# Attention output projection of the second pass: from one level of seven products to two, over pairs of key/value groups

## The chip, the cores and the metric

The kernel runs on one core of one Trainium2 chip. The metric is device time in microseconds (us) of one execution. A core has five engines that run side by side and wait for each other by semaphores: PE (TensorE, the matrix products; PEld is its weight load), DVE (VectorE), ACT (ScalarE), POOL (GpSimd) and SP (SyncE, which here issues DMA transfers). A profile of one execution shows when each instruction ran.

## The reference

The reference is two layers of a gated network over x of 8 sequences of 256 tokens, 1024 wide, in fp32. The part that matters is the second layer's attention, with 32 query heads and 8 key/value heads (so 8 groups of 4 query heads), all heads 128 wide:

```python
q = (query @ wq).reshape(bs, s, N_Q_HEADS, D_K).transpose(0, 2, 1, 3)
k = (key @ wk).reshape(bs, s, N_KV_HEADS, D_K).transpose(0, 2, 1, 3)
v = (value @ wv).reshape(bs, s, N_KV_HEADS, D_V).transpose(0, 2, 1, 3)
q = _rope(q)
k = _rope(k)
qg = q.reshape(bs, N_KV_HEADS, g, s, D_K)
scores = jnp.einsum('bhgqd,bhkd->bhgqk', qg, k) / scale
masked = jnp.where(mask[:, None, None].astype(bool), scores, -1000000000.0)
w = jax.nn.softmax(masked, axis=-1)
out = jnp.einsum('bhgqk,bhkd->bhgqd', w, v)
out = out.reshape(bs, N_Q_HEADS, s, D_V).transpose(0, 2, 1, 3).reshape(bs, s, N_Q_HEADS * D_V)
return out @ wo
...
x = x + jnp.tanh(g_xattn[1]) * _L1_xattn_ref(_layernorm(x, axis=-1), ctx_4096, ctx_4096, ...)
```

The change concerns `out @ wo`, the product of 4096 columns of attention output with the 4096 x 1024 matrix `wo`.

## The kernel before

The kernel makes two passes (`NPASS`), each over four sequences, that is 1024 rows of x, which stay on chip as eight tiles of 128 rows. A pass has four stages: an autocorrelation layer with the keys and values of the later attention computed beside it, a feed-forward layer (`lora_ffn`), the attention, and a second feed-forward layer (`fourier_ffn`).

Most large products use the seven-product scheme for 2 x 2 block matrices (Winograd's form): in place of eight block products there are seven, whose operands are sums of blocks (`left_operands`, `right_operands`) and whose results are added into the four result blocks. The products are named 1, 2, 6, 7, 4, 5, 3 and run in this order (`SEVEN`). Product 1 opens a running sum u, products 2, 6, 7, 5 and 3 add to it or to its copy w, and product 5 is used twice.

The attention runs 16 steps in each pass: two blocks of 512 rows (two sequences) by eight groups. A step k has four units (n, l): n is the sequence, l a half of the group's four heads. In each unit:

- `scores` multiplies queries by keys (line 977), then masks (986), reduces (988), exponentiates on ACT (991) and scales (1000) the weights of two heads.
- `values`, for the unit before, transposes the weights (1012), multiplies by the values (1023) and copies the result to a tile oT (1031).
- In between, PE is given other products from two generators: `queries` (929), the seven query products of the next step, and `outputs` (958), the seven output products of the step before. `q_fill` and `o_fill` (lines 1046 and 1047) say how many of each fall into each unit.

One output product of a step is [two row tiles] x [256 of the step's 512 columns of attention output] x [512 of the 1024 result columns]: two matmuls of 128 x 512 for each of the two row tiles. So a step has 7 x 2 x 2 = 28 matmuls. The result in PSUM is scaled by the gate and added into x or a partial sum by `add_product` (257 to 267, and `residual`, 375), on ACT, DVE and POOL.

Operands of the left side are made by POOL from the oT tiles (206 to 209). Operands of the right side are sums of blocks of `wo`: in the first block of the first pass they are made on chip by DVE and stored in DRAM (`wo_d`), and in the other blocks loaded (`load_wo`), seven tiles of 512 KB a step, into a group of seven buffers (`go`). `wq` is treated in the same way (group `gq`). PSUM tiles of the query and output products come from one pool of four buffers (`at_mm`).

`combine` evicts the query products and hands four finished blocks to `rope`, which multiplies them by tables on DVE (720 to 722) and adds on POOL (723).

The program is written in one order and then put into a fixed order for each engine's queue by a scheduler at build time; each queue runs in that order and waits where it must. SP issues nearly all DMA transfers.

Of the kernel before, what the change touches and what calls it, by code (L numbers as in the profile page):

```python
# [11 lines left out]
F32 = mybir.dt.float32  # L12
# [34 lines left out]
def flamingo_kernel(ctx: ExitStack, tc: tile.TileContext, a: dict, out: bass.AP):  # L47
# [26 lines left out]
    tab = const.tile([P, 2, S], F32, name="tab")  # L74
# [4 lines left out]
    def load_constants():  # L79
        nc.sync.dma_start(tab, a["rope"])  # L80
# [20 lines left out]
    ]  # L101

# [117 lines left out]
    def combine(r, ps, tiles, new, dest):  # L220
# [11 lines left out]
        elif r == 7:  # L232
            tiles["w"] = new("w")
            nc.vector.tensor_add(tiles["w"], ps, tiles["u"])
        elif r == 5:
# [478 lines left out]
    def rope(dst, ps, cos, sin, pool):  # L714

        H = P // 2
        t0 = pool.tile([P, 2, S], F32, tag="rope0", name="rope0", bufs=1)
        t1 = pool.tile([P, 2, S], F32, tag="rope1", name="rope1", bufs=1)
        tab = lambda t: t.unsqueeze(1).to_broadcast([t.shape[0], 2, S])
        nc.vector.tensor_mul(t0, ps, tab(cos))  # L720
        nc.vector.tensor_mul(t1[0:H], ps[H:P], tab(sin[H:P, :]))
        nc.vector.tensor_mul(t1[H:P], ps[0:H], tab(sin[0:H, :]))  # L722
        nc.gpsimd.tensor_add(dst, t0, t1)  # L723

    def keys_values(n, groups, pools):
# [105 lines left out]
    def query_operands(xt, norm, pool, ps_t, tag):  # L831
# [4 lines left out]
        for t in range(NBT):  # L836
            xn = pool.tile([P, D], F32, tag="xn", name="xl")
# [8 lines left out]
        return right_operands(nc.vector, q, *s)  # L846

# [3 lines left out]
    def attention(p, xt, gq, go, keep, norms, xops):  # L851
        with (
# [7 lines left out]
            wq, wo, kv = {}, {}, {}  # L860

# [22 lines left out]
            def load_wo(step):  # L884
# [12 lines left out]
                else:  # L897
                    ops = {}
                    where = {1: a["wo"][g, 0, 0], 2: a["wo"][g, 1, 0], 3: a["wo"][g, 1, 1]}
                    where |= dict(zip((5, 7, 6, 4), wo_d[g]))  # L900
                    for r in SEVEN:
                        ops[r] = big_tile(go, [2, HALF], f"wo_{r}")
                        nc.sync.dma_start(ops[r], where[r])
                wo[step] = ops

            def load_kv(step):
                blk, g = step
                r0 = p * BP * S + blk * NB
                kT = w2.tile([P, NB], F32, tag="kv", name="kT", bufs=4)
                nc.sync.dma_start(kT, kT_d[g, :, r0 : r0 + NB])  # L910
                v = w2.tile([P, NBT, DH], F32, tag="kv", name="v", bufs=4)
# [9 lines left out]
            def queries(step, qT):  # L921
# [3 lines left out]
                for r in SEVEN:  # L925
# [10 lines left out]
                    done = combine(r, ps, tiles, lambda tag: half(tag, 1), lambda: half("c", 2))  # L936
                    if done:
                        qT[done[1]] = half("qT", 8)
                        rope(qT[done[1]], done[0], tab_q[:, 0, :], tab_q[:, 1, :], w1)
                    yield  # L940

            def outputs(step, ops):
# [11 lines left out]
                for r in SEVEN:  # L954
                    for t in range(2):
# [10 lines left out]
                        add_product(r, po, x[t], tg_x[1], ntg_x[1], flat)  # L966
                    yield
# [38 lines left out]
            def values(step, l, n, got, oT, fill):  # L1006
# [23 lines left out]
                oT[n][l] = half("oT", 8)  # L1030
# [5 lines left out]

            load_wq(steps[0])
# [6 lines left out]
            last, before, nothing = None, None, iter(())  # L1044

            q_fill = {0: (2, 2, 1, 1), len(steps) - 1: (0, 0, 0, 0)}
            o_fill = {len(steps) - 1: (2, 2, 2, 1)}
            oT = [[None, None], [None, None]]
            for k, step in enumerate(steps):
# [9 lines left out]
                o_gen = nothing  # L1059
                for i, (n, l) in enumerate(((0, 0), (0, 1), (1, 0), (1, 1))):  # L1060
                    got = scores(step, l, n, qT)
                    nq = q_fill.get(k, (3, 3, 1, 0))[i]
                    no = o_fill.get(k, (0, 1, 3, 3))[i]
                    fill_from(q_gen, nq)
                    if i > 0:
                        fill_from(o_gen, no - 1)
                    if before is not None:
                        values(*before, lambda: fill_from(o_gen, 1 if no else 0))
                    before = step, l, n, got, oT
                    if i == 0 and k > 0:  # L1070
                        s = [half(f"oS{j}", 1) for j in (1, 2, 4)]
                        o_gen = outputs(last[0], left_operands(nc.gpsimd, last[1], *s))
                        fill_from(o_gen, no)
# [6 lines left out]
                    if i == 0:  # L1080
                        load_wo(step)
                for gen in (q_gen, o_gen):
                    for _ in gen:
                        pass
# [278 lines left out]
```

## Time and profile before

| | us |
|---|---|
| median of 3 runs | 3401.2 (3400.71 to 3402.15) |
| the profiled execution | 3396.83 |
| its span, first to last instruction | 3395.0 |
| second pass's attention, first query product to last output product | 2226.5 to 3281.9 |
| one step in the middle of it | 65.65 |
| output products after the last step | 22.6 |

In the lines of the profile a group is written: line, engine, operation, out<-in, shape and count; then its busy time in us and the mean of one in ns; then the idle time of its engine just before it and what ended that. A matmul of these fp32 operands appears as two records. The chain of waits is followed back from the last instruction: each piece is the work, or the wait, that held up the next one. Pieces in order of time give start, length and what ran. A table by windows gives the busy time of each engine in a stretch of time.

The page lists 160526 packets and 425.17 MB on the queue that SP feeds, 36.3% of the time of 16 DMA engines.

### The profile page before, as it was taken

Reading aid. Unit: us, or ns where it says so; the run is one execution under the profiler, and the core shown is the slowest. Engines: PE = TensorE matmul, PEld = TensorE weight load, DVE = VectorE, ACT = ScalarE, POOL = GpSimd, SP = SyncE. Lnnn points to the kernel's source line nnn. Section 1 sums busy time; section 2 is a strip of 40 time slices with the busy share of each in tenths; the row PEclk is TensorE's granted clock in tenths of the full one; section 3 lists DMA queues with packets and bytes.
Section 4 is the critical chain, followed back from the end, with each engine's and each line's share of the span. In section 5 each row is a group of like instructions: output and inputs, shape, how many; then the busy total and the mean of one; then the engine's idle time right before and its main releaser. Section 6 shows DMA issues by size and latency. Waiting matters only on the chain. (4 is left out here: it accounts for less than half of the span.)

```text
span 3395.0 us, 36926 instructions
## 1 busy us (share of the span) xinstructions
PE 3314.1 (98%) x12784; PEld 2279.1 (67%) x12784; DVE 2252.4 (66%) x4229; ACT 859.7 (25%) x2061; POOL 1354.6 (40%) x1213
## 2 busy tenths in 40 slices
PE   8899999999999999999999999999999999999999
PEld 6566546767767776775467766577767776776654
DVE  7787666877777666665657775556666666666563
ACT  1233111322222222222123321112222322222220
POOL 4665212344443443344335542123443444344332
PEclk9999999999999999999999999999999999999999
DMA  7433634333333333343153424053333333333411
GB/s 270 170 115 102 207 115 155 130 140 127 137 127 131 121 119 123 118 155 118 56 196 130 147 96 146 17 173 115 118 125 120 115 118 121 121 118 122 158 44 50
DMA packets 161864, 431.72 MB, mean 127 GB/s; under 512 B 21476, under 2 KB 56292, under 8 KB 161678
## 3 DMA queue, kind: packets, MB, share of 16 engines
q1 hardware_dynamic: 160526, 425.17, 36.3%
q0 software_dynamic: 1152, 4.19, 0.3%
q8 instruction: 102, 1.67, 0.2%
q14 instruction: 84, 0.69, 0.1%
HBM read 350.66 MB, written 78.64 MB: 126 GB/s over the span
## 5 line engine op out<-in xcount | busy, mean ns | idle before, releaser
L723 POOL TENSOR_TENSOR qT<-rope,rope 128x512 f32<-128x512 f32 x128 | 170.2, 1330 | 867.5 <-DVE rope L722 867.5
L958 PE MATMUL po<-wo,oT 128*128 128x512 f32 x960 | 432.1, 593 | 0.0
L929 PE MATMUL ps_q<-xn,wq 128*128 128x256 f32 x1920 | 428.9, 379 | 0.0
L375 DVE SCALAR_TENSOR_TENSOR x<-po,tg,x 128x512 f32<-128x512 f32 x376 | 269.1, 745 | 196.0 <-PE po L958 70.5
L929 PEld LDWEIGHTS ps_q<-xn,wq 128*128 128x128 f32 x1920 | 364.8, 190 | 50.5 <-PE po L682 0.5
L991 ACT ACTIVATE s<-s,nmx 128x256 f32<-128x256 f32 x512 | 256.0, 501 | 277.0 <-DVE nmx L988 276.5
L986 DVE COPY_PREDICATED s<-keep,ps_s 128x512 f32<-128x512 uint8 x256 | 185.9, 729 | 182.2 <-PE ps_s L977 177.7
L958 PEld LDWEIGHTS po<-wo,oT 128*128 128x128 f32 x960 | 177.4, 190 | 175.6 <-issue 170.5
L958 PE MATMUL po<-wo,oS 128*128 128x512 f32 x640 | 287.7, 592 | 0.3 <-DVE x L375 0.3
L929 PE MATMUL ps_q<-xn_t,wq 128*128 128x256 f32 x1280 | 285.6, 379 | 0.0
L1018 ACT COPY wT<-pt 128x512 f32<-128x512 f32 x256 | 138.1, 590 | 515.9 <-PE pt L1012 515.7
L929 PEld LDWEIGHTS ps_q<-xn_t,wq 128*128 128x128 f32 x1280 | 243.2, 190 | 33.1
L1023 PE MATMUL av<-wT,v 128*128 128x256 f32 x1024 | 246.2, 383 | 5.1 <-ACT wT L1018 5.1
L977 PE MATMUL ps_s<-kT,qT 128*128 128x256 f32 x1024 | 247.9, 379 | 0.0
L1023 PEld LDWEIGHTS av<-wT,v 128*128 128x128 f32 x1024 | 191.4, 190 | 80.0 <-issue 44.0
L1000 DVE TENSOR_SCALAR s<-s,tot 128x256 f32<-128x256 f32 x512 | 220.0, 470 | 7.7
L985 POOL MEMSET s<- 128x512 f32 x256 | 130.0, 527 | 220.7 <-PE pt L1012 219.0
L958 PEld LDWEIGHTS po<-wo,oS 128*128 128x128 f32 x640 | 118.9, 190 | 136.7 <-issue 128.9
L977 PEld LDWEIGHTS ps_s<-kT,qT 128*128 128x128 f32 x1024 | 191.6, 190 | 25.3 <-DVE x L375 0.5
L258 POOL TENSOR_TENSOR x<-x,part 128x512 f32<-128x512 f32 x80 | 109.1, 1364 | 229.5 <-ACT part L257 222.1
L988 DVE TENSOR_REDUCE nmx<-s 128x2 f32<-128x512 f32 x256 | 175.0, 685 | 8.3
L263 POOL TENSOR_TENSOR x<-x,part 128x512 f32<-128x512 f32 x80 | 104.7, 1310 | 172.7 <-DVE part L375 157.0
(257 smaller groups left out, 5594.0 us busy)
## 6 DMA issues: line engine op xcount, KB each, us to landing
wq<-in_wq_dram SPq DMA_DIRECT2D x104, 512.0 KB, 3.2
wo<-in_wo_dram SPq DMA_DIRECT2D x104, 512.0 KB, 3.2
wq<-wq_d SPq DMA_DIRECT2D x96, 512.0 KB, 3.2
wo<-wo_d SPq DMA_DIRECT2D x96, 512.0 KB, 3.2
w<-w_d SPq DMA_DIRECT2D x36, 512.0 KB, 4.8
wk<-in_wk_dram SPq DMA_DIRECT2D x26, 512.0 KB, 5.9
wv<-in_wv_dram SPq DMA_DIRECT2D x26, 512.0 KB, 3.8
wk<-wk_d SPq DMA_DIRECT2D x24, 512.0 KB, 4.5
```

The costliest lines, as they stand in the source:

```text
L375: nc.vector.scalar_tensor_tensor(xs, ps, g, xs, ALU.mult, ALU.add)
L723: nc.gpsimd.tensor_add(dst, t0, t1)
L929: nc.tensor.matmul(ps[:, l, :], wops[r][:, l, c, :], xo[r][:, c, :], start=(c == 0), stop=(c == KH - 1),)
L958: nc.tensor.matmul(po, ops[r][:, h, t * P : (t + 1) * P], wops[r][:, h, :], start=(h == 0), stop=(h == 1),)
L977: nc.tensor.matmul(ps[:, t, :], qT[i, n][:, l, t * P : (t + 1) * P], kT[:, n * S : (n + 1) * S], start=True, stop=True,)
L985: nc.gpsimd.memset(s, MASKED)
L986: nc.vector.copy_predicated(s, keep[b], ps)
L988: nc.vector.tensor_reduce(nmx, s, AX.X, ALU.max, negate=True)
L991: nc.scalar.activation(s[:, t, :], s[:, t, :], AF.Exp, bias=nmx[:, t : t + 1], accum_out=tot[:, t : t + 1],)
L1000: nc.vector.tensor_scalar(s[:, t, :], s[:, t, :], tot[:, t : t + 1], None, ALU.mult)
L1018: nc.scalar.copy(wT[i], pt)
L1023: nc.tensor.matmul(av[:, i, :], kv[step][1][:, n * 2 + c, :], wT[i][:, c, :], start=(c == 0), stop=(c == 1),)
```

## The change

In the second pass (`paired`) the output projection no longer works step by step. Two steps (a pair of groups, 1024 columns of attention output) are taken together, and each of the seven first-level products is itself computed by seven products (r2) one level down: the rows are split again (256 into 128), the two groups of the pair are the split of the inner dimension, and the result columns are split again (512 into 256). A pair then has 49 products of two matmuls of 128 x 256 (`outputs_of_two`). Their results are added up in PSUM-sized quarters: u (`o_u`) and v (`o_w`) are single buffers, c collects the four result quarters of one first-level product, and after its last product the two halves of c are added into x by POOL or DVE.

Operands of the second level on the left (`finer`) are made by POOL from slices of oT, four for each first-level product, while the product before it runs. On the right, the second-level sums of each first-level operand over the two groups are computed in the first pass, second block, for odd groups (`finer_weights`): two sums on DVE and two on POOL for each of the seven operands, stored in DRAM (`wo2_d`). To have both groups' operands on chip, two of seven tiles of an odd group come from buffers of their own. In the second pass `stream_wo` loads them, with slices of the first-level operands, through the same seven buffers.

Also changed: the keys' rope table is loaded in each pass into a pool of that stage; `rope` works in place with one temporary; the query blocks are written straight into qT tiles (seven buffers, not eight); in the second pass product 5 of the queries is evicted by two DVE additions in place of an ACT copy and two POOL additions; kT and v have three buffers, not four; normalized rows for the second block's queries come from the ring `xn`; the fill tables differ by pass, with outputs of a pair spread over the two steps that follow it.

```diff
-    tab = const.tile([P, 2, S], F32, name="tab")
...
+    wo2_d = [dram.tile([P, 7, 2, 2, 2, S], F32, name=f"wo2_d{i}") for i in range(N_KV // 2)]
...
+        elif r == 5 and alone:
+            c = dest()
+            nc.vector.tensor_add(c, ps, tiles["w"])
+            nc.vector.tensor_add(tiles["u"], ps, tiles["u"])
+            return c, (1, 1)
...
-        nc.vector.tensor_mul(t0, ps, tab(cos))
-        nc.vector.tensor_mul(t1[0:H], ps[H:P], tab(sin[H:P, :]))
-        nc.vector.tensor_mul(t1[H:P], ps[0:H], tab(sin[0:H, :]))
-        nc.gpsimd.tensor_add(dst, t0, t1)
+        nc.vector.tensor_mul(t[0:H], x[H:P], tab(sin[H:P, :]))
+        nc.vector.tensor_mul(t[H:P], x[0:H], tab(sin[0:H, :]))
+        nc.vector.tensor_mul(dst, x, tab(cos))
+        nc.gpsimd.tensor_add(dst, dst, t)
...
+            xn = new()
...
+            paired = p == NPASS - 1
...
+                    for n, r in enumerate(SEVEN):
+                        if g % 2 and n < 2:
+                            ops[r] = w1.tile([P, 2, HALF], F32, tag="wo", name=f"wo_{r}", bufs=2)
+                        else:
+                            ops[r] = big_tile(go, [2, HALF], f"wo_{r}")
+                        nc.sync.dma_start(ops[r], wo_operand(g, r))
...
+            def finer_weights(step):
+                blk, g = step
+                for n, r in enumerate(SEVEN):
+                    w = wo[blk, g - 1][r], wo[step][r]
+                    q = [[w[k][:, :, j * S : (j + 1) * S] for j in range(2)] for k in range(2)]
+                    t67, t45 = (
+                        w1.tile([P, 2, 2, S], F32, tag=f"fine_{i}", name=f"fine_{i}")
+                        for i in ("t67", "t45")
+                    )
+                    nc.vector.tensor_sub(t45[:, 1], q[0][1], q[0][0])
+                    nc.vector.tensor_sub(t67[:, 1], q[1][1], q[0][1])
+                    nc.gpsimd.tensor_sub(t67[:, 0], q[1][1], t45[:, 1])
+                    nc.gpsimd.tensor_sub(t45[:, 0], t67[:, 0], q[1][0])
+                    nc.sync.dma_start(wo2_d[g // 2][:, n, 0], t67)
+                    nc.sync.dma_start(wo2_d[g // 2][:, n, 1], t45)
+                    yield
...
+            def stream_wo():
+                places = []
+                for _, g in steps[::2]:
+                    for n, r in enumerate(SEVEN):
+                        q = [
+                            [wo_operand(g + k, r)[:, :, j * S : (j + 1) * S] for j in range(2)]
+                            for k in range(2)
+                        ]
+                        d = wo2_d[g // 2][:, n]
+                        places += [(q[0][0], q[1][0]), d[:, 0], d[:, 1], (q[1][1],)]
+                tiles = []
+                for n, src in enumerate(places):
+                    for coming in places[len(tiles) : n + 7]:
+                        tiles.append(big_tile(go, [2, 2, S], "wo"))
+                        if isinstance(coming, tuple):
+                            for i, part in enumerate(coming):
+                                nc.sync.dma_start(tiles[-1][:, i], part)
+                        else:
+                            nc.sync.dma_start(tiles[-1], coming)
+                    for i in range(len(src) if isinstance(src, tuple) else 2):
+                        yield tiles[n][:, i]
...
-                kT = w2.tile([P, NB], F32, tag="kv", name="kT", bufs=4)
+                kT = w2.tile([P, NB], F32, tag="kv", name="kT", bufs=3)
...
+            def outputs_of_two(blk, qs):
+                g, ng = tg_x[1], ntg_x[1]
+                tiles = lambda t, i: xt[blk * NBT + i * 2 + t]
+                x = [
+                    [
+                        [tiles(t, i)[:, j * HALF : (j + 1) * HALF] for j in range(2)]
+                        for i in range(2)
+                    ]
+                    for t in range(2)
+                ]
+                s1 = [half("oT", 13) for _ in qs]
+                for q, s in zip(qs, s1):
+                    nc.gpsimd.tensor_add(s, q[1][0], q[1][1])
+                    nc.gpsimd.tensor_sub(q[1][0], q[0][0], q[1][0])
+                at = lambda i, k: [q[i][k] for q in qs]
+                ops = {1: at(0, 0), 2: at(0, 1), 6: at(0, 0), 7: at(1, 0), 4: at(1, 1), 5: s1}
+                ops[3] = ops[2]
...
+                def finer(r):
+                    q = [[o[:, :, t * P : (t + 1) * P] for o in ops[r]] for t in range(2)]
+                    made = {1: q[0][0], 2: q[0][1], 4: q[1][1]}
+                    def make():
+                        for i, (op, y, z) in {
+                            5: (nc.gpsimd.tensor_add, q[1][0], q[1][1]),
+                            7: (nc.gpsimd.tensor_sub, q[0][0], q[1][0]),
+                            6: (nc.gpsimd.tensor_sub, 5, q[0][0]),
+                            3: (nc.gpsimd.tensor_sub, q[0][1], 6),
+                        }.items():
+                            made[i] = w2.tile([P, 2, P], F32, tag="oI", name=f"oI{i}", bufs=8)
+                            op(made[i], *(made[v] if isinstance(v, int) else v for v in (y, z)))
+                            yield
+                    return made, make()
...
+                for n, r in enumerate(SEVEN):
+                    coming = finer(SEVEN[n + 1]) if r != SEVEN[-1] else ({}, iter(()))
+                    g1, g2 = (ng, g) if r == 4 else (g, ng)
+                    c = [half("co", 6) for t in range(2)]
+                    for r2 in SEVEN:
+                        w = next(wo_stream)
+                        po = ps_mm.tile([P, S], F32, tag="mm", name="po")
+                        for h in range(2):
+                            nc.tensor.matmul(
+                                po, left[r2][:, h, :], w[:, h, :], start=(h == 0), stop=(h == 1)
+                            )
+                        scaled = nc.vector.scalar_tensor_tensor
+                        if r2 == 1:
+                            u = quarter("o_u", 1)
+                            nc.scalar.activation(u, po, AF.Copy, scale=g1)
+                        elif r2 == 2:
+                            scaled(c[0][:, 0, :], po, g1, u, ALU.mult, ALU.add)
+                        elif r2 == 6:
+                            scaled(u, po, g1, u, ALU.mult, ALU.add)
+                        elif r2 == 7:
+                            v = quarter("o_w", 1)
+                            scaled(v, po, g1, u, ALU.mult, ALU.add)
+                        elif r2 == 4:
+                            scaled(c[1][:, 0, :], po, g2, v, ALU.mult, ALU.add)
+                        elif r2 == 5:
+                            scaled(c[1][:, 1, :], po, g1, v, ALU.mult, ALU.add)
+                            scaled(u, po, g1, u, ALU.mult, ALU.add)
+                        elif r2 == 3:
+                            scaled(c[0][:, 1, :], po, g1, u, ALU.mult, ALU.add)
+                        if r2 in (1, 2, 6, 7):
+                            next(coming[1], None)
+                        if r2 != 3:
+                            yield
...
+                        if r == 1:
+                            add(nc.gpsimd, x[t][0][0])
+                        elif r == 2:
+                            add(nc.vector, x[t][0][0])
+                        elif r == 6:
+                            add(nc.vector, part[t])
+                            nc.gpsimd.tensor_add(x[t][0][1], x[t][0][1], part[t])
+                        elif r == 7:
+                            nc.vector.tensor_add(ct, ct, part[t])
+                            add(nc.gpsimd, x[t][1][0])
+                            add(nc.gpsimd, x[t][1][1])
+                        elif r == 4:
+                            add(nc.gpsimd, x[t][1][0])
+                        elif r == 5:
+                            add(nc.gpsimd, x[t][0][1])
+                            add(nc.gpsimd, x[t][1][1])
+                        elif r == 3:
+                            add(nc.vector, x[t][0][1])
+                    if r == 1:
+                        part = [y.rearrange("p b s -> p (b s)") for y in c]
+                        for q, s in zip(qs, s1):
+                            nc.gpsimd.tensor_sub(q[0][0], s, q[0][0])
+                    elif r == 2:
+                        for q in qs:
+                            nc.gpsimd.tensor_sub(q[0][1], q[0][1], q[0][0])
+                    left = coming[0]
...
+            if paired:
+                q_fill = {0: (2, 2, 1, 1), 1: (2, 2, 2, 1), end: (0, 0, 0, 0)}
+                o_fill = {k: (0, 5, 10, 10) if k % 2 == 0 else (3, 5, 8, 8) for k in range(end)}
+                o_fill[end] = (6, 6, 6, 6)
+            else:
+                q_fill = {0: (2, 2, 1, 1), end: (0, 0, 0, 0)}
+                o_fill = {k: (0, 1, 3, 3) for k in range(end)}
+                o_fill[end] = (2, 2, 2, 1)
+            middle = 4 if paired else 1
...
+                    if i == 0 and p == 0 and step[0] > 0 and step[1] % 2:
+                        fine = finer_weights(step)
+                    fill_from(fine, 2 if k == end else 1)
```

## The prediction

> **What bounds the kernel now.** I read the page first: its busy line and slices.
>
> ```profile
> PE 3314.1 (98%) x12784; PEld 2279.1 (67%) x12784; DVE 2252.4 (66%) x4229; ACT 859.7 (25%) x2061; POOL 1354.6 (40%) x1213
> ...
> PE   8899999999999999999999999999999999999999
> ```
>
> PE is busy everywhere. [...] I took the chain of waits over one step of the second pass's attention (2951.8 to 3017.4).
>
> ```profile
> 2951.76 1.73 PE ps_s L977 x8
> 2953.48 10.36 PE ps_q L929 x48
> ...
> 2978.66 0.87 PE pt L1012 x8
> 2979.53 3.44 PE po L958 x8
> 2982.97 1.73 PE av L1023 x8
> 2984.69 1.73 PE ps_s L977 x8
> 2986.42 3.45 PE ps_q L929 x16
> 2989.87 6.87 PE po L958 x16
> ```
>
> Every piece is PE and each begins where the last ended. L929 (moving 256 columns) takes 10.36 / 48 = 215.9 ns a record, L958 (512 columns) 6.87 / 16 = 429.4; a product has two records. The step is 65.65 us: queries 24.17, outputs 24.05, scores 6.9, values 6.9, transposes 3.6, and no gap. Here PE time saved is time saved, if the others keep up. How much room they have is in the windows:
>
> ```profile
> 762.00:827.70 65.70, 65.70 (x265) 47.33 (x264) 50.64 (x80) 17.83 (x48) 28.65 (x26) 1.00 0.38 136
> 2951.60:3017.20 65.60, 65.60 (x265) 47.29 (x264) 41.14 (x71) 17.84 (x48) 26.50 (x26) 1.00 0.36 120
> 3214.20:3259.30 45.10, 45.10 (x172) 28.86 (x171) 28.75 (x55) 17.92 (x49) 17.92 (x18) 1.00 0.30 102
> 3259.30:3281.90 22.60, 22.60 (x55) 9.91 (x53) 11.10 (x16) 1.96 (x3) 14.84 (x12) 1.00 0.00 0
> ```
>
> Columns: window, PE, weight loads, DVE, ACT, POOL, clock, DMA share, GB/s. The first row is a step of pass 1 with DVE at 50.6 of 65.7 and the same step length: 77% of DVE does not slow PE. The second is the step above, then the last step, then the tail. Prices come from the groups:
>
> ```profile
> L375 DVE SCALAR_TENSOR_TENSOR x<-po,tg,x 128x512 f32<-128x512 f32 x376 | 269.1, 745 | 196.0 <-PE po L958 70.5
> L929 PEld LDWEIGHTS ps_q<-xn,wq 128*128 128x128 f32 x1920 | 364.8, 190 | 50.5 <-PE po L682 0.5
> L207 POOL TENSOR_TENSOR oT<-oT 128x512 f32<-128x512 f32 x32 | 40.9, 1278 | 2.5
> L296 POOL TENSOR_TENSOR co<-co,mf 128x320 f32<-128x320 f32 x3 | 2.6, 864 | 1.3 <-DVE mf L295 1.3
> ```
>
> **What the skill says.** "TensorE: Matmul & The Clock Gate", section "Step-by-step: what each phase is for", says that PE pulls the next weight load ahead of running matmuls. The trace agrees for the very shape that the change uses: a 190 ns load a record fits in L929's 216 ns. "VectorE: DVE Perf Modes", "TRN2 errata", prices an fp32 tensor_tensor at (N+151)/0.96 ns, 691 at 512; the trace has 691 (L720). "SBUF — State Buffer", "SBUF: two separate sides", says that DVE operations with two SBUF inputs, or in a 2-port mode, and GpSimd operations exclude each other for a whole instruction. The trace agrees: the 128x256 multiply L1000 has a median of 352 ns and a maximum of 1428 in pass 2.
>
> **The change, part by part.**
>
> *PE.* A pair of groups had 2 x 28 matmuls of 512 columns: 56 x 2 x 429.4 = 48.09 us. Now it has 49 x 2 of 256: 98 x 2 x 215.9 = 42.31. That is 5.78 saved a pair, 46.3 for eight pairs, all on the path. No other PE work changes.
>
> *DVE, a pair.* Removed: 28 evictions x 0.745 = 20.9. Added: 49 evictions of 256 columns. The 512-column one holds 533 ns of elements at the rate of the cited formula, so 267 go: 0.478 each, 23.4. (As bounds: 0.42, the tensor_tensor formula; 0.66, L588 at 128x256, which also accumulates.) Added: 8 sums x 0.69 = 5.5, and r=5 of the queries, which takes two DVE adds a step for an ACT copy and two POOL adds: 2.8. Net +10.8 a pair, 46.5 of 62.8 a step, 74%: under the 77% shown harmless.
>
> *POOL, a pair.* Removed: 16 adds into x and 4 of the queries, x 1.27. Added: 14 adds (17.8) and 28 half-size operand sums. From L296 and L207, 2.15 ns an element gives 0.73 each, 20.4. Net +12.8: 32.9 of 62.8 a step. They are made one first-level product (6 us of PE) ahead, into eight buffers, and so lie beside its matmuls; without that cover PE would wait up to 2.9 us (four sums) at each. The eight full-size sums of two groups stay eight. ACT is even.
>
> *Weights.* A pair streamed 14 x 0.524 MB, now 28 tiles of which seven are half filled: 12.8 MB. A step goes from 7.9 to 10.6 MB, 169 GB/s, about half the DMA time at the trace's ratio; the first slice of the page reaches 270 GB/s. Seven buffers lie six tiles (10 us of products) ahead; a 512 KB wo tile lands in 3.2 us. SP's queue holds wq, kT/v and wo loads in the order in which PE frees their buffers. v now waits for the step's last scores, but is read a unit and a half later; its issue holds up nothing that PE needs before then. Cost nothing; a tile that is late costs PE what is left of its 3.2 us.
>
> *Pass 1.* In four pairs of steps, 14 DVE sums (9.7 us), 14 on POOL (18) and 14 writes of 512 KB: over 131 us. DVE goes from 41.1 to about 46 of 65.6 a step, POOL from 26.5 to 36, and PE is not touched. The writes stand on SP's queue and wait there for POOL; behind them wait loads of wq and wo that PE reads a step (65 us) later or, for wo, at least a unit (13 us) later. That slack hides them. Zero; upper bound 3 us.
>
> *Rope, tab, qT, xl.* Same three DVE multiplies and one POOL add; tab is loaded twice. The xl tiles now share the ring of seven and free themselves within the step. Zero, up to 1 us.
>
> *What is late next.* (a) Slots of the PSUM ring (four) now turn over every 0.86 us, not 1.72, and r=5 is read twice, with rope multiplies between in the compiled DVE order. In an even step's third unit, counted from the end of scores: DVE is done with softmax at 4.5, the query eviction at 5.2, r5's first read 5.7, two rope multiplies 7.1, its second read 7.6. PE has filled four slots by 6.0 and a fifth at 6.9 and needs r5's: 0.7 us late, then 0.4 for r3's. With port clashes 1.5 a pair, six pairs: 9 us. Bounds 3 and 20. (b) Steps 0 and 1 now have no output products between: step 1 runs like step 0, whose gaps come to about 1 us: +1. (c) The last step has 24 products and no queries: units of 9.5 us of PE against about 9 of DVE (softmax 5.05, six evictions 2.9, sums 0.7): +2 (0 to 5). (d) The tail is 42.3 us of products alone; POOL has some 40 us of work in it, and DVE adds 0.69 to x after the last eviction: +2 (0 to 5).
>
> **Sum** against the profiled execution, 3396.8 (span 3395.0): -46.3 + 9 + 1 + 2 + 2 = -32.3, so 3364.5. The median of the runs shown is 4.4 above the profiled one: 3401.2 - 32.3 = 3369.
>
> **Rivals.** *All hidden:* -42 to -46, 3355 to 3359. For it: the present step has no gap at all, and so does the one with DVE at 77%. Against: the ring is half as deep in time. *Half given back:* -7 to -20, 3381 to 3394, if the evictions cost 0.66 (+9 us of DVE a pair) and POOL's extra 28 operations hold the shared port before DVE's. For it: L1000's maximum. Against: evictions read PSUM and one SBUF operand. *The saving is not there* (within 7 us of 3401): if a product of 256 columns cost more than half of one of 512. L929 speaks against it. *Slower:* DVE takes over in the bursts of ten products. One unit (13.0 us of PE) now holds 11 us of DVE. o_u has one buffer, so ACT cannot open the next first-level product before DVE closes the last, and any excess goes to PE whole. There are 56 such products. Behind the waiting ACT eviction stand the exponentials and the copies that PE's transposes and values wait for. The saving is gone at 0.83 us lost in each, 1.2 in a unit of ten; DVE would need 14.2 us there, that is 0.8 an eviction, or 3 us of port waits in a unit. At 0.95 each it gives 3408. Against: 0.745 is the price of twice the columns.
>
> **How the numbers follow.** Forecast (-20 to -42) 0.65; all hidden 0.14; half given back 0.10; no saving 0.03; slower 0.08. A measurement here tells 0.2%, 6.8 us, from no change. So faster 0.89, same 0.03, slower 0.08. The range 3354 to 3388 takes in all hidden and most of half given back, and leaves out about 0.15.
>
> **What would show it.** The second pass's outputs at 216 ns between records and 42.3 us a pair; a pair of steps of 125.5 us plus one to two; gaps of PE in front of the sixth and seventh products after a query product, ended by DVE; evictions of 0.48. It is wrong if POOL's operand sums or the wo loads end PE's waits, or if pass 1 grows longer.

## The result, and the profile after

The changed kernel takes 3383.3 us (median of 5 runs, 3382.4 to 3390.0) against 3401.2 before, a ratio of 0.995 with a 95% interval of 0.9936 to 0.9965. That is 17.9 us less, inside the forecast's range, and about half of the 32.3 it named. The profiled execution took 3383.27 us with a span of 3381.5, 13.5 under the span before. The trace splits this by stages (from the first scores of an attention to its last output product, and what lies around):

| us | start to first attention | attention, pass 1 | between the two | attention, pass 2 | rest | span |
|---|---|---|---|---|---|---|
| before | 590.3 | 1032.1 | 631.6 | 1027.9 | 113.1 | 3395.0 |
| changed | 583.4 | 1049.2 | 638.1 | 996.7 | 114.1 | 3381.5 |
| difference | -6.9 | +17.1 | +6.5 | -31.2 | +1.0 | -13.5 |

Each row is one profile. The same code of pass 1's attention runs in three profiles of this study (the changed kernel, experiments 9 and 11), and takes 1049.2, 1048.6 and 1049.1 us in them, so the 17.1 us are no scatter. The second pass gained nearly what was forecast, and the first pass's attention, which should not have moved, gave more than half of it back. First the page of the changed kernel:

```profile
PE 3278.5 (97%) x13456; PEld 2411.3 (71%) x13456; DVE 2396.7 (71%) x4549; ACT 854.1 (25%) x2069; POOL 1559.5 (46%) x1445
```

PE's busy time fell by 35.6 us. The page's slices are 85 us each and hide gaps of a few us; stretches show them. This is the table by windows of the changed kernel (window, length, PE, weight loads, DVE, ACT, POOL, clock, DMA share, GB/s): an odd step of pass 1, a pair of steps of pass 2, the last step, the tail.

```profile
1153.00:1222.00 69.00, 66.00 (x266) 47.34 (x266) 51.99 (x90) 20.47 (x51) 36.31 (x32) 1.00 0.45 153
2864.60:2992.20 127.60, 126.21 (x614) 110.58 (x614) 97.03 (x188) 37.84 (x100) 68.45 (x74) 1.00 0.52 168
3184.40:3230.00 45.60, 45.60 (x231) 40.09 (x230) 36.70 (x74) 18.81 (x52) 32.86 (x36) 1.00 0.53 174
3230.00:3267.40 37.40, 37.40 (x175) 32.92 (x173) 26.05 (x53) 2.84 (x6) 37.01 (x38) 1.00 0.75 246
```

The step of pass 1 is 69.0 us long where it was 65.7, with PE busy for 66.0 of it. The pair of pass 2 takes 127.5 us (131.3 before), and PE lacks 1.4 us of it. The last step and the tail have no gap at all.

Who PE waited for in pass 1's attention (engine, line, releaser: us in total, times, longest):

```profile
PE po L1015 <- DVE x L381: 9.4, 6, 3.0
PE av L1188 <- ACT wT L1183: 5.6, 3, 2.4
PE pt L1177 <- DVE s L1165: 1.8, 1, 1.8
```

The output products wait for DVE's additions into x. In the kernel before, the waits listed for that attention add up to 4.9 us (4.2 of them for wT), here to 16.8. PE is busy for 1032.2 of its 1049.2 us, before for 1027.2 of 1032.1, so some 12 of the 17.1 us are idle time of PE and some 5 are work that took longer. Part of these 5 is the clock, which is granted in full all through that attention before, and here is not in two stretches at the ends of waits of 2.6 and 2.5 us (same columns, the clock is third from the end):

```profile
1353.30:1356.70 3.40, 3.03 (x4) 1.48 (x5) 3.40 (x6) 0.00 (x0) 1.03 (x1) 0.50 0.49 161
1489.80:1493.20 3.40, 3.40 (x7) 1.68 (x6) 3.40 (x7) 0.00 (x0) 1.96 (x3) 0.50 0.35 117
```

PE works for 6.4 us in them, at half the clock, which makes about 3.2 us lost (an estimate from these two lines).

What DVE itself waited for, over the second block of that attention:

```profile
DVE fine_t L932 <- DMA wo_d<-fine_t: 20.7, 8, 3.3
DVE fine_t L931 <- DMA wo_d<-fine_t: 17.5, 11, 4.6
```

DVE stood in front of the two sums of `finer_weights` that it makes. One such place, on DVE's timeline (start, length; in brackets the idle time before it):

```profile
1213.43 0.15 DVE L1163 RECIPROCAL tot<-tot 128x2 f32<-128x2 f32 x1
1216.49 0.69 DVE L932 TENSOR_TENSOR fine_t<-wo,wo 128x512 f32<-128x512 f32 x1 [2.90 <-issue]
1217.10 0.61 DVE L1165 TENSOR_SCALAR s<-s,tot 128x256 f32<-128x256 f32 x2
1217.62 0.74 DVE L381 SCALAR_TENSOR_TENSOR x<-po,ntg,x 128x512 f32<-128x512 f32 x1
```

and on POOL's at the same time:

```profile
1207.88 1.72 POOL L273 TENSOR_TENSOR x<-x,part 128x512 f32<-128x512 f32 x1
1209.56 1.27 POOL L272 TENSOR_TENSOR x<-x,part 128x512 f32<-128x512 f32 x1
1210.79 1.28 POOL L273 TENSOR_TENSOR x<-x,part 128x512 f32<-128x512 f32 x1
1212.02 1.35 POOL L933 TENSOR_TENSOR fine_t<-wo,fine_t 128x512 f32<-128x512 f32 x1
```

Read them from the bottom. POOL's sum of the round before (L933) stood behind a row of additions into x and ended at 1213.4. Only then could its tile be written; the write was issued at 1213.39, and such writes take 3.1 us to land (the page's list of transfers has that median). That makes 1216.5, and at 1216.49 DVE went on: there is one buffer of the tile, and it was free. (For this wait the profile names no releaser, it says "issue"; for most of the others it names the write.) Behind the waiting sum stood the evictions (L381), and PE stood from 1215.4 to 1218.4, when the first of them had freed its PSUM slot.

### The profile page after: what moved, and what is told of

It is laid out like the page before. It is cut to its first block, busy times and chain, and to the rows that moved or that the text cites. A ratio compares the mean times of both kernels' runs of the same rounds, so it can differ in the third digit from the quotient of the medians.

```text
span 3381.5 us, 39786 instructions
## 1 busy us (share of the span) xinstructions
PE 3278.5 (97%) x13456; PEld 2411.3 (71%) x13456; DVE 2396.7 (71%) x4549; ACT 854.1 (25%) x2069; POOL 1559.5 (46%) x1445
## 5 line engine op out<-in xcount | busy, mean ns | idle before, releaser
L728 POOL TENSOR_TENSOR qT<-qT,rope 128x512 f32<-128x512 f32 x128 | 169.6, 1325 | 685.6 <-DVE qT L727 685.6
L381 DVE SCALAR_TENSOR_TENSOR x<-po,tg,x 128x512 f32<-128x512 f32 x248 | 176.8, 743 | 113.1 <-PE po L688 42.2
L1165 DVE TENSOR_SCALAR s<-s,tot 128x256 f32<-128x256 f32 x512 | 236.1, 501 | 7.1
L1078 PE MATMUL po<-wo,oI 128*128 128x256 f32 x896 | 217.1, 382 | 9.4 <-POOL oI L1061 8.3
L1015 PE MATMUL po<-wo,oT 128*128 128x512 f32 x448 | 201.5, 592 | 0.0
L1078 PEld LDWEIGHTS po<-wo,oI 128*128 128x128 f32 x896 | 167.6, 190 | 38.0 <-POOL oI L1061 11.8
L1150 POOL MEMSET s<- 128x512 f32 x256 | 128.2, 526 | 129.4 <-PE pt L1177 121.8
L264 POOL TENSOR_TENSOR x<-x,part 128x512 f32<-128x512 f32 x48 | 68.0, 1417 | 221.0 <-ACT part L263 221.0
L1078 PE MATMUL po<-wo,oT 128*128 128x256 f32 x672 | 167.6, 380 | 2.0 <-DVE co L1093 2.0
L1196 ACT COPY oT<-av 128x512 f32<-128x512 f32 x128 | 74.9, 585 | 370.9 <-PE av L1188 370.9
```

Of the source, the lines that this page charges most:

```text
L381: nc.vector.scalar_tensor_tensor(xs, ps, g, xs, ALU.mult, ALU.add)
L728: nc.gpsimd.tensor_add(dst, dst, t)
L1015: nc.tensor.matmul(po, ops[r][:, h, t * P : (t + 1) * P], wops[r][:, h, :], start=(h == 0), stop=(h == 1),)
L1078: nc.tensor.matmul(po, left[r2][:, h, :], w[:, h, :], start=(h == 0), stop=(h == 1))
L1165: nc.vector.tensor_scalar(s[:, t, :], s[:, t, :], tot[:, t : t + 1], None, ALU.mult)
```

## The experiments

An edit is put in order anew by the scheduler when the kernel is built, so an edit in one place can move instructions beside it. The lengths of stages in a profile are therefore compared as well as the medians; each comes from one profiled execution. The runs are spread over four chips, on which the kernel before took 3390.4 to 3402.4 us, so medians are compared with those of kernels beside them. In experiments 1 and 4 to 6, where no complete sums are stored, the second pass reads other stored tiles of the same size in their place; these lines are not shown.

**1. Without the sums.**

```diff
-                    if i == 0 and p == 0 and step[0] > 0 and step[1] % 2:
+                    if False:
                         fine = finer_weights(step)
...
```

> Left out: the sums of finer_weights and their writes in the first pass (the second pass then streams other stored tiles of the same size, so its output is not the reference's). The changed kernel loses 18 us in the first pass's attention against the kernel before, which my forecast put at zero. Theory W (finer_weights makes DVE wait): all or nearly all of the 18 comes back, 3363 to 3368, and the first pass's steps are 65.65 us again. Rival O (the other edits in that stage: three kT/v buffers, seven qT buffers, two parked tiles, rope in place): 3379 to 3384, the steps stay long. If the 18 us split, the part that stays is O's.

Measured: 3361.5 us beside a kernel before of 3390.4, ratio 0.9902 (0.9883 to 0.992). Pass 1's attention takes 1030.8 us. All of the loss belongs to `finer_weights`; the other edits of that stage cost nothing (1032.1 before).

**2. Two buffers of half the size.**

```diff
-                    q = [[w[k][:, :, j * S : (j + 1) * S] for j in range(2)] for k in range(2)]
...
-                        w1.tile([P, 2, 2, S], F32, tag=f"fine_{i}", name=f"fine_{i}")
...
+                    for h in range(2):
+                        q = [[w[k][:, h, j * S : (j + 1) * S] for j in range(2)] for k in range(2)]
...
+                            w1.tile([P, 2, S], F32, tag=f"fine_{i}", name=f"fine_{i}", bufs=2)
...
```

> The sums of finer_weights are made in halves (128x256) with two buffers for each of the two tiles in the place of one: same memory, same elements, twice the instructions (28 more on DVE and 28 more on POOL a pair). Theory W: DVE's in-order queue stood at the first sum of a round until the write of the round before had landed, so with a second buffer 10 to 18 us come back, 3366 to 3373. Rival L (load: the sums take DVE's time or the port from the evictions): more instructions make it the same or worse, 3383 to 3390.

Measured: 3382.0 us beside 3390.4, and 1051.9 us in that attention, no gain. W in its first form fails, yet not in favour of L: DVE still stands before the sums (31.1 us for the writes and 10.7 for POOL's sums, in the second block). In data, two halves are no deeper than one whole tile; that this is why nothing was gained was not tried.

**3. All sums on POOL.**

```diff
-                    nc.vector.tensor_sub(t45[:, 1], q[0][1], q[0][0])
-                    nc.vector.tensor_sub(t67[:, 1], q[1][1], q[0][1])
+                    nc.gpsimd.tensor_sub(t45[:, 1], q[0][1], q[0][0])
+                    nc.gpsimd.tensor_sub(t67[:, 1], q[1][1], q[0][1])
```

> All four sums of a round on POOL, one buffer as in the changed kernel. Now POOL waits for the write, and DVE never does. Theory W: the 18 us come back as far as POOL is not late itself, 3366 to 3374. Rival L with the port (POOL's instructions shut DVE out): POOL has 18 us more a pair, 3383 to 3390. If POOL's own queue becomes late (its additions into x free nothing that PE needs soon), 3375 to 3383.

Measured: 3397.2 us, ratio to the kernel before 1.0014 (1.0002 to 1.0027), and 1062.2 us in that attention. This is slower than all three expectations. DVE waits for none of the sums here, but 41.3 us for POOL's clearing of the tiles s (L1150), and PE waits for DVE's evictions and once, 3.4 us, for an operand of POOL's. So POOL is the engine that is late, and its lateness also reaches PE by other ways than the sums' one buffer.

**4 to 6. The parts of finer_weights one by one.** No writes (the last two of these lines are left out); no writes and no sums on POOL (all four left out); no sums on POOL with the writes of DVE's half kept (all four left out, and `t67[:, 1]` and `t45[:, 1]` written).

```diff
-                    nc.gpsimd.tensor_sub(t67[:, 0], q[1][1], t45[:, 1])
-                    nc.gpsimd.tensor_sub(t45[:, 0], t67[:, 0], q[1][0])
-                    nc.sync.dma_start(wo2_d[g // 2][:, n, 0], t67)
-                    nc.sync.dma_start(wo2_d[g // 2][:, n, 1], t45)
```

> Left out: the writes of finer_weights to DRAM (its sums are made on DVE and POOL as before; the second pass streams other stored tiles). Read from the length of the first pass's attention: 1032.1 us in the kernel before, 1049.2 in the changed one, 1030.8 without the sums. Theory W1 (DVE waits for the write of the round before, some 3 us after POOL's last sum): 1031 to 1036. Theory W2 (DVE waits for POOL's sums of the round before, which stand behind POOL's additions into x): 1042 to 1049. Theory L (DVE's own 0.69 us a sum is too much in these units): 1046 to 1049.

> Left out: the writes and POOL's two sums of each round; DVE's two sums stay, and wait for nothing but their operands (the second pass streams other stored tiles). Theories W1 and W2: 1031 to 1034. Theory L: 1044 to 1049, since DVE's load is the same as in the changed kernel.

> Left out: POOL's two sums of each round and their half of the writes; DVE's two sums are written, each tile's half by itself. DVE then waits only for a write that starts as soon as it is done itself. W1 alone: about half of the loss stays, 1036 to 1046. W2 alone: 1031 to 1034. L: 1044 to 1049.

Measured, pass 1's attention, one execution each: 1076.5 without the writes, 1030.8 with DVE's sums alone, 1031.3 with DVE's sums and their writes. With POOL's sums gone, neither DVE's sums (L) nor the writes of its half (W1) cost anything; POOL's two sums are what costs (W2). Without the writes, what DVE and PE waited for (first lines of each answer):

```profile
DVE fine_t L931 <- POOL fine_t L934: 53.0, 21, 4.2
...
PE po L1013 <- POOL s L1148: 27.8, 3, 9.3
```

and the windows of the step's fourth unit, without writes

```profile
1202.00:1218.00 16.00, 12.19 (x43) 7.19 (x41) 7.98 (x9) 1.68 (x5) 15.84 (x14) 1.00 0.31 102
```

and with DVE's sums alone:

```profile
1202.00:1218.00 16.00, 16.00 (x52) 9.02 (x52) 13.34 (x24) 3.85 (x11) 10.90 (x9) 1.00 0.41 135
```

In the first POOL is busy for 15.84 of 16 us and DVE for 8; in the second DVE is the busier, 13.3, and PE is never short. In these two units it matters less how full an engine is than who stands behind it. DVE's 53.0 us show that link itself: it waits for POOL's sum. (PE's wait is put down to POOL's clearing of s, but in the first of the three DVE's eviction L381 ended at 1223.39, and PE went on at 1223.49.) The runs take POOL's sums away as a whole, its work and DVE's wait for it together; that the loss goes through DVE's queue is read from the traces.

That the run without writes is worse than the changed kernel itself was expected by no theory. Its order is another one, with POOL fuller in that unit, and that was not tried apart. The trace has one more part of it: four stretches of 10.2 us, 41.0 in all, in which the granted clock is 0.50. The first begins inside PE's wait of 9.3 us:

```profile
1218.00:1228.20 10.20, 4.71 (x6) 2.16 (x7) 9.93 (x16) 2.04 (x6) 3.70 (x5) 0.50 0.05 20
```

Its attention has 39.2 us of PE's idle time (17.0 in the changed kernel), and PE's busy time is 5.1 us longer.

**7. Other units for the sums.**

```diff
-                    fill_from(fine, 2 if k == end else 1)
+                    fill_from(fine, 2 if k == end else ((2, 2, 1, 0), (1, 1, 0, 0))[k % 2][i])
```

> The whole of finer_weights, seven rounds a pair as in the changed kernel, but asked for in the units that hold few output products: 1, 1, 0, 0 in an odd step and 2, 2, 1, 0 in the even step after it, in place of one in each unit. The lost time of the changed kernel lies at the end of the fourth unit of odd steps. If the coincidence of the sums with the additions into x on POOL is what counts (W2): first pass's attention 1033 to 1042, 3367 to 3376. If the rounds wait as long in their new place (W1 or L): 1046 to 1055, 3380 to 3390.

Measured: 3376.4 us beside 3390.8, and 1045.2 us in that attention, a gain of 4, just under the second expectation. The sums need the operands of both groups on chip, so they can't move far, and the waits stay (DVE before L931 for writes 21.5 us; PE idle for 16.3 us, 17.0 in the changed kernel). What went is the half clock: that attention has no such stretch in this run, and PE's busy time is 3.4 us shorter. So the move is not shown to ease the waits.

**8. Before with the new rope.** The body of `rope` as in the changed kernel, nothing else.

> The kernel before with one edit: rope as in the changed kernel (two half multiplies first, then the full one into the destination, POOL adds in place). In the first stage of pass 1 the two kernels run the same DVE and POOL instructions in the same order but for rope, yet the changed one gains 6.9 us there and loses 5.7 in the first stage of pass 2. Theory P (a shift of some 0.3 us decides whether one DVE instruction meets a train of back-to-back POOL instructions: 11.23 us for 128x256 in the kernel before): the time of each first stage moves by 3 to 9 us either way; if as in the changed kernel, -7 and +6, about 3400. Rival T (the table's new place and load time): nothing moves, 3401 with both first stages as before.

Measured: 3392.6 us beside 3390.4, ratio 1.0004 (0.9992 to 1.0016). The first stage took 584.3 us (590.3 in the kernel before), the stretch between 632.3 (631.6). Half of P's expectation came, which tells little; experiment 9 settles the first stage.

**9. The changed kernel again.**

> The changed kernel once more, beside the kernel before, because the first stages of both passes moved by up to 8 us between profiles of kernels whose first stages are the same. By theory P (one DVE instruction that starves behind POOL's train, or not): first stage 582 to 585 us or 588 to 590, the stretch between the two attentions 631 to 633 or 635 to 638, and the attentions 1049 and 997 each time. Median 3374 to 3384, against a kernel before of 3388 to 3392 as in the runs above. If those stages were changed by the edits: 583.4 and 638.1 again.

Measured: 3389.6 us beside 3401.0, ratio 0.9965 (0.9953 to 0.9976), 11.4 us less. Both kernels are slower than expected here. The attentions took 1048.6 and 995.8 us, as in the first profile; the first stage 590.4, not 583.4, with the very same program. So the 6.9 us were no work of the change. The stretch between took 638.4 us, close to the 638.1 of the first profile, as the rival had it. In this profile DVE's timeline has

```profile
121.92 11.61 DVE L594 SCALAR_TENSOR_TENSOR w<-took,ex 128x256 f32<-128x256 f32 x1
```

where the first profile of the same kernel has

```profile
121.34 0.75 DVE L594 SCALAR_TENSOR_TENSOR w<-took,ex 128x256 f32<-128x256 f32 x1
```

One instruction took 11.6 us (the median of its 64 like is 0.43), and PE waited 6.8 us behind it; from 131.9 to 138.7 the granted clock was 0.50. POOL meanwhile, in the run with 11.61:

```profile
120.90 1.30 POOL L442 TENSOR_TENSOR odr<-ma,mb 128x512 f32<-128x512 f32 x1
122.15 1.30 POOL L444 TENSOR_TENSOR odi<-ma,mb 128x512 f32<-128x512 f32 x1
...
130.75 2.50 POOL L159 TENSOR_TENSOR wv_s<-wv,wv_s 128x512 f32<-128x512 f32 x2
```

DVE's instruction, with two operands in SBUF, ended at 133.53, just after POOL's unbroken row (133.25). Of the fourteen profiles of this study (before, changed, and one of each run here), the six in which this instruction lost 9.7 us or more have a first stage of 588.5 to 590.4 us, and the eight others 582.0 to 585.1, whichever kernel it is. The stretch between the attentions varies too, from 631.5 to 639.8, also among kernels that differ from the changed one only inside an attention; the profiles over 633 all have one DVE instruction (L477) stalled by 8.4 us near its middle, but one with 631.8 has that too, so its 6.5 us stay open.

**10. All sums on DVE.**

```diff
-                    nc.gpsimd.tensor_sub(t67[:, 0], q[1][1], t45[:, 1])
-                    nc.gpsimd.tensor_sub(t45[:, 0], t67[:, 0], q[1][0])
+                    nc.vector.tensor_sub(t67[:, 0], q[1][1], t45[:, 1])
+                    nc.vector.tensor_sub(t45[:, 0], t67[:, 0], q[1][0])
```

> All four sums of a round of finer_weights on DVE, none on POOL; writes as in the changed kernel. Theory W2 (DVE waits for POOL's sums, which stand behind the additions into x): first pass's attention back to 1031 to 1037 of 1049, that is 12 to 18 us under the changed kernel beside it, 3360 to 3368. Rival L2 (DVE gets too full: 14 more sums of 0.69 us a pair, up to 56 of 66 us in odd steps, and the write of one round, 3.1 us, still stands before the next): 1042 to 1055, no gain.

Measured: 3374.2 us, 15.4 under the changed kernel beside it, ratio to before 0.9928 (0.9915 to 0.994). Pass 1's attention takes 1036.4. This is W2's number for the stage; the whole lies above its 3360 to 3368, since the kernels beside it are slower as well. With DVE fuller than ever in that unit

```profile
1202.00:1218.00 16.00, 16.00 (x54) 9.23 (x53) 15.53 (x25) 3.74 (x11) 8.80 (x8) 1.00 0.59 214
```

PE has no gap. The median gained more than that stage (12.8 us); the first stages differ between runs. 4.3 us over the kernel before remain in that attention: PE is idle for 8.0 us of it (4.9 before), most of them in waits for wT (6.1; 4.2 before). What causes them was not tried.

**11. Pass 2 without rope's half multiplies.** The chain of waits of the changed kernel, in the third unit of an even step:

```profile
2903.80 0.88 PE po L1078 x4
...
2907.18 1.18 POOL oI L1061
2908.36 0.02 issue
2908.38 2.10 PE po L1078 x8
```

It names POOL's operand sum. DVE's timeline there:

```profile
2904.90 0.48 DVE L1095 SCALAR_TENSOR_TENSOR co<-po,tg,o_w 128x256 f32<-128x256 f32 x1
2905.40 0.69 DVE L725 TENSOR_TENSOR rope<-qT,tab_q 64x512 f32<-64x512 f32 x1
2906.10 1.66 DVE L726 TENSOR_TENSOR rope<-qT,tab_q 64x512 f32<-64x512 f32 x1
2907.80 0.48 DVE L1096 SCALAR_TENSOR_TENSOR o_u<-po,tg,o_u 128x256 f32<-128x256 f32 x1
```

The second read of product 5 (L1096) ends at 2908.28, and PE starts at 2908.38: two candidates within 0.1 us.

```diff
-                        rope(done[0], done[0], tab_q[:, 0, :], tab_q[:, 1, :], w1)
+                        if paired:
+                            cos = tab_q[:, 0, :].unsqueeze(1).to_broadcast([P, 2, S])
+                            nc.vector.tensor_mul(done[0], done[0], cos)
+                            nc.gpsimd.tensor_add(done[0], done[0], done[0])
+                        else:
+                            rope(done[0], done[0], tab_q[:, 0, :], tab_q[:, 1, :], w1)
```

> Left out: in the second pass's queries, rope's two half multiplies on DVE (POOL adds the tile to itself, so its load stays). Read from the second pass's attention, 996.7 us from first scores to last output product. The profile puts PE's wait of 1.29 us a pair down to POOL's operand sums (oI). My forecast's mechanism D: PE waits for the PSUM slot of product 5, whose second read on DVE stands behind two rope multiplies. D: the waits of 1.29 and 0.42 us in each pair go, 984 to 989. Rival S (POOL's sums are late): they stay, 993 to 997.

Measured: pass 2's attention takes 984.6 us, and this is all that PE waited for in it:

```profile
PE po L1083 <- DVE co L1098: 2.0, 1, 2.0
PE po L1083 <- issue: 0.2, 1, 0.2
```

The waits went with the multiplies while POOL's sums stayed: D, and not S. (DVE also has eight multiplies of 0.69 us or more less a step in this kernel, so that any other lateness of DVE's evictions would shrink too.)

**12. Both mends.** The sums on DVE as in 10, and

```diff
-                    nq = q_fill.get(k, (3, 3, 1, 0))[i]
+                    nq = q_fill.get(k, (3, 4, 0, 0) if paired else (3, 3, 1, 0))[i]
```

> Both mends in one kernel that computes everything: the sums of finer_weights all on DVE as in the run before, and in the second pass the query products are spread 3, 4, 0, 0 over the four units of a step in place of 3, 3, 1, 0, so that no query product, and no rope, falls into a unit with ten output products. Mechanism D (the slot of product 5 waits behind rope on DVE): the second pass's attention goes from 996 to 983 to 988 us, the whole to 3358 to 3368 with a first pass's attention of about 1036. Rival U (the third unit has too little PE work ahead of ten evictions and the softmax without its query product, so that PE waits there for DVE instead): 994 to 1010.

Measured: 3370.0 us, ratio to the kernel before beside it 0.9899 (0.9882 to 0.9915), the best of the kernels that compute everything. Pass 1's attention takes 1035.9 us. Pass 2's takes 991.7, 5.0 us less where experiment 11 gave 12.1, between the two expectations. The wait of 1.29 us a pair fell to 0.24, but in odd steps a new one of 1.16 stands in place of the 0.42, behind another eviction (these waits are counted from start to start, less 0.216 us a record; the views count them up to 0.16 shorter):

```profile
PE po L1078 <- DVE co L1086: 6.0, 6, 1.0
```

That is the third unit, which has no query product now; DVE stood there in two scalings of weights (L1165, 3.03 us at 2838.99), which take 0.62 at 2902.51 in the changed kernel. So U has its part as well.

## Why the prediction was right, and where it was wrong

The direction and the range were right; the gain was sized at 32.3 us and came out at 17.9. That is short of the forecast's own -20 to -42, and inside the range only because the range took in most of a rival, half given back (3381 to 3394), and not by that rival's causes: the evictions cost 0.48 us, not 0.66, and the loss lies in pass 1. Luck has a part as well. The loss in pass 1 was put at nothing, and the profile's first stage happened to be 6.9 us shorter; the same program run again was 11.4 us faster than the kernel before beside it, not 17.9. By its steps:

- *PE's saving, 46.3 us.* Right. Records of the new products are 216.0 ns apart, 42.3 us a pair.
- *DVE's evictions, 0.478 us each.* The groups have 0.473 to 0.484. The bound of 0.66, on which the rival rested, was misread: L588's mean of 0.659 holds the one stalled instruction of 11.23 us, and its median is 0.43. *POOL's half-size sums, 0.73:* 0.77 to 0.91, of no effect. *Weights, cost nothing:* no wait of PE on a load in pass 2's attention.
- *(a) Slots of the PSUM ring, 9 us.* Right in place and mechanism, too small in size: about 2.0 us a pair (1.29 and 0.42, and some of 0.1) in place of 1.5, and seven pairs with it, not six. The larger part fits the port: the half multiply that I priced at 0.69 took 1.66 us in that unit of 13 steps of the pass, each time beginning 0.6 us after an addition of POOL's (L1105) and ending 0.5 us after it, where port clashes were priced at some 0.4 us a pair. In the list of what would show it wrong I had POOL's sums, and the chain of waits does name them; experiment 11 says it is DVE and the ring.
- *(b), (c), (d), 5 us together.* Too large for the first two steps (no gap over 0.11 us; 1 forecast) and the last (no gap; 2 forecast), about right for the tail (the wait after it grew from 2.45 to 3.7 us). The change of block cost 2.2 us where it cost 0.6 before; that was not foreseen. Pass 2 and the rest changed by -30.2 us against the -32.3 of the sum.
- *Pass 1: "Zero; upper bound 3 us".* This is the step that failed: +17.1 us. That pass 1 grows longer was in the list of what would show the forecast wrong. I compared averages over a pair of steps (POOL 36 of 65.6 us, DVE 46) and checked only who waits for the writes on SP's queue. I did not ask who waits for POOL. DVE's sum of a round needs a tile that POOL's sum of the round before has read and a write has emptied, and there is one of it; in the fourth unit of an odd step POOL has a row of additions into x first. DVE waits in its queue, its evictions with it, and PE behind them. Averages over 131 us can't show a unit of 16 us in which an engine is full. Experiments 5 and 6 (DVE's sums without POOL's: no loss) and 10 (all on DVE: 12.8 us back) show that POOL's sums are the cause; the way through DVE's queue is read from the traces. A clock of 0.50 after two of the waits adds some 3 us, which the forecast has no term for.
- *The first stages, not in the sum at all.* -6.9 and +6.5 us in the two profiles. The first is a difference between executions of one program (experiment 9); the second is open.

The other rivals fell: the saving is there, and DVE did not take over the bursts.

## What to carry to other kernels

When work is split over two engines with one buffer between them, ask which queue each half stands in, and what is ahead of it there in that very stretch: a slow engine that nobody waits for costs nothing, a fast one that waits for it hands the delay on to all that is queued behind. It can be cheaper to give all of such work to the engine that has the critical evictions than to share it; here the loss was 4.3 us in place of 17.1. And when a wait's releaser is named by the profile, look for a second candidate that ended within 0.1 us of it.

## What the runs showed of the hardware

The Trainium skill, "SBUF — State Buffer", section "SBUF: two separate sides", says that a GpSimd operation and a DVE operation with two SBUF inputs exclude each other for a whole instruction. In one place it was more than one: a DVE instruction of 128x256 took 11.6 us and ended 0.3 us after POOL's whole unbroken row, and not after the instruction that was running. In another it was one: rope's half multiply (L726 at 2906.10) ended 0.5 us after POOL's addition L1105, and POOL's next instruction (L1061, back to back with it) took 1.17 us, where 0.72 is the shortest of its like. What decides whether DVE gets in is not shown: over the fourteen profiles the stalled instruction started between 121.50 and 122.69 us, and where it was not stalled between 121.34 and 122.69. With the stall the first stage took 588.5 to 590.4 us, without it 582.0 to 585.1. Whether this is also what spreads the times of one kernel from run to run is not shown, since one run of each was profiled.

The granted clock of PE fell to 0.50 around some of PE's waits, for 3.4 us (at the ends of waits of 2.5 and 2.6), 6.8 us (around one of 6.8) or 10.2 us (around one of 9.3), but not around the wait of 3.0 us that ended at 1218.4. Under it four records of an output product took 3.47 us, elsewhere 1.88. So a wait can cost more than its own length.
